# The head of a two-layer attention kernel: the second image's statistics and norm moved ahead in the order of work

## The chip, the cores and the metric

The kernel runs on one core of one Trainium2 chip. The metric is the device time of one execution in microseconds (us). Before the change it was 2573.52 us, the median of three runs (2573.21 to 2574.76).

The core's engines work side by side, each through a queue of its own: PE is the matmul engine (its weight loads are listed as PEld), DVE the vector engine, ACT the scalar engine, POOL the general engine, and SP issues most of the transfers between the chip's memory and the core's.

## What is computed

Two attention layers over a batch of eight images of 512 channels by 1024 pixels, the second on the first one's output. The first layer, cut to what matters:

```python
h = group_norm(xf, gn_w, gn_b)                   # 32 groups of 16 channels
qkv = jnp.einsum('oc,bct->bot', qkv_w, h) + qkv_b[None, :, None]
q, k, v = jnp.split(qkv.reshape(b * NUM_HEADS, -1, T), 3, axis=1)
q, k, v = fake_quant(q), fake_quant(k), fake_quant(v)   # 8 bits, range over the whole tensor
w = softmax(jnp.einsum('bct,bcs->bts', q * scale, k * scale))
a = jnp.einsum('bts,bcs->bct', w, v)
return xf + jnp.einsum('oc,bct->bot', proj_w, a.reshape(b, c, T)) + proj_b[None, :, None]
```

The second layer is a group norm, one head of attention over 512 channels, a projection and the residual. Since `fake_quant` needs the smallest and the largest value of q, k and v over all images, the kernel first computes q, k and v of all eight images and stores them. This is its phase 1, and it takes until about 580 us. The change lies in its first hundred microseconds.

## The kernel before

**Precision.** [...] Weights and x are therefore split into `high`, `low` and `mix`, three tiles of the fast type: `high` by ACT, then `low` (a subtraction) and `mix` (one fused operation) by DVE. For the weights a further ACT operation scales `low`. `split_half(b, hf)` gives the six steps of an image's half, three for each half of the channels: ACT, DVE, DVE. `split_weights` gives `first` (ACT), `second` (both DVE operations) and `third` (ACT). The list `parts` holds four of these: `parts[0]` for half of the q weights, `parts[1]` for half of the k weights, and `parts[2]` and `parts[3]` for v. The split of an image takes the buffer of an earlier one: two are kept, and `raw_w`, the unsplit weights, is in the first.

**A block.** `three` runs twelve matmuls into two PSUM banks: `w_high` by `high` and `w_low` by `low` into bank `a`, and the `mix` pair into bank `m`. `put` brings them out: for q and k, ACT scales `a` into one of three `u` tiles and DVE joins `u` with `m` and takes the largest value; for v, DVE does both. After two blocks `store` takes the smallest value on DVE (TENSOR_REDUCE) and issues the store. The `ps_1` pool has eight banks for everything in phase 1.

**Image 0.** Some of its q and k is done directly in fp32 by `qk_mm` (the tiles `early`, `late` and `last`), while the splits are being made; `out_of` brings these out with the bias and `keep` stores them. What remains are eight blocks for each half of its pixels: two of q, two of k, four of v (`blocks`, the branch `b == 0`). The other images have twelve blocks a half.

**The biases.** The norm's offset goes through the weights into the biases. `bias(i)` is a generator in two steps for q, k and v (`bq`, `bk`, `bv`). Its first step runs eight narrow matmuls into `wt` and copies them to `stage` on ACT; its second sums them by matmuls (`wc` for q and k, `wr` for v) and adds on DVE.

**The norm of the following images.** `norm_steps` takes statistics of each of four channel groups on DVE (two BATCH_NORM_STATS2 and one aggregate, then a `yield`), averages the means over the groups by a matmul (`gps`), forms offsets on DVE, averages these by a second matmul (`gps2`), and forms scale and offset on DVE with a power on POOL between. `apply` then scales x in place on ACT, a channel group at a time.

**The order.** In phase 1 the calls on DVE and ACT are tied in the order in which the program makes them (`InOrder`), and so are the matmuls (`mm`). So the text is the order of each of the three queues, for images 0 and 1; from image 2 on DVE and ACT are placed by the compiler's scheduler, and SP's transfers always are. The head is written out call by call, and after it the loop over images and halves runs a block and then gives each generator in `side` one step (`go`). In image 0's first half these are `chores`, which has the rest of `bv`, the stores of `last` and the last steps of `second`, and `every_second(ahead)`, which takes one step of image 1's norm on every second block: four statistics in eight blocks. In the second half `ahead` goes on, a step a block, and after the third block it is drained and the split of image 1's first half begins, a step a block. What is left of `side` at the end of a half is drained.

The lines the change and the steps of the prediction touch are the function `norm`, the statements from `first = split_half(0, 0)` to `next(bv)`, the generators after it, and the loop `for b in range(B)`.

Of the kernel before, what the change touches and what calls it, by code (L numbers as in the profile page):

```python
# [19 lines left out]
B, C, HH, WW = 8, 512, 32, 32  # L20
T = HH * WW
CC = C // P
NT = T // P
NH = T // 512
# [34 lines left out]
def attn_pair_kernel(  # L59
# [12 lines left out]
    class InOrder:  # L72
# [10 lines left out]
        def after(self, ins):  # L83

            tc.add_manual_dep(self.latest, ins.name, IN_ORDER, reason="order")
# [69 lines left out]
    dve, act, pe = InOrder(nc.vector), InOrder(nc.scalar), InOrder(nc.tensor)  # L155
# [52 lines left out]
    def mm(ps, lhsT, rhs, **kw):  # L208
        ins = nc.tensor.matmul(ps, lhsT=lhsT, rhs=rhs, **kw).ins  # L209
        part = lhsT.shape[-1] / P if lhsT.shape[-1] in (32, 64) else 1.0  # L210
        if rhs.dtype in (BF, F16, F32R):
            part *= 0.25 * lhsT.shape[0] / P
        pe.t += math.prod(rhs.shape[1:]) * 1.677e-3 * part
        if last_mm[0] is not None:
            tc.add_manual_dep(ins, last_mm[0].name, IN_ORDER, reason="order")
        last_mm[0] = ins

    def stat_tiles(n, nm):
        return (
            small.tile([P, n, NH, 6], F32, tag=f"gst{n}", name=f"gst_{nm}"),  # L220
            small.tile([P, n, 2], F32, tag=f"gmv{n}", name=f"gmv_{nm}"),
        )

    def aggregate(mv, st, i):
        dve.bn_aggr(mv[:, i, :], st[:, i, :, :].rearrange("p a s -> p (a s)"))
# [81 lines left out]
    with ExitStack() as fast:  # L307
# [84 lines left out]
        with tc.tile_pool(name="p1w", bufs=1) as p1w, tc.tile_pool(  # L392
# [7 lines left out]
            xs, halves = {}, {}  # L400
# [43 lines left out]
            def split_half(b, hf):  # L444
                halves[b, hf] = t = p1.tile(
                    [P, 3, CC, 512], F32R, tag="half", name=f"half_{b}_{hf}"
                )
                steps = []
                for k in (slice(0, CC // 2), slice(CC // 2, CC)):
                    high, low, mix = (t[:, i, k, :] for i in range(3))  # L450
                    src = xs[b][:, k, bass.ts(hf, 512)]
                    steps += [
                        lambda high=high, src=src: act.activation(
                            high, src, AF.Identity, scale=NUDGE
                        ),
                        lambda high=high, low=low, src=src: dve.tensor_tensor(
                            low, src, high.bitcast(F32), ALU.subtract
                        ),
                        lambda high=high, low=low, mix=mix: dve.scalar_tensor_tensor(
                            mix, low.bitcast(F32), -SH, high.bitcast(F32), ALU.mult, ALU.add  # L460
                        ),
                    ]
                return steps
# [3 lines left out]
                    step()  # L467
                    yield

            def norm(b):  # L470

                xt = xs[b]

                def apply(cc, scale, off):
                    act.activation(xt[:, cc, :], xt[:, cc, :], AF.Identity, bias=off, scale=scale)

                return norm_steps(
                    lambda cc, hf: xt[:, cc, bass.ts(hf, 512)], None, V_GN0W, one, f"a{b}",
                    fine=True, apply=apply,
                )  # L480

            out_ring = wa.rearrange("p s k n -> p (s k n)")
# [5 lines left out]
            def turn_of(name, n):  # L488
                turns[name] += 1
                return (turns[name] - 1) % n  # L490

            def out_tile():
                i = turn_of("out", 3)
                return out_ring[:, i * 1024 : (i + 1) * 1024].rearrange("p (a n) -> p a n", a=2)
# [73 lines left out]
            def bias(i):  # L568


                by_channel, by_row = weigh(
                    one, stage[i % 2][:, 512:1024] if i == 0 else stage[1][:, 0:512],
                    lambda e: raw_w[:, e, bass.ts(i, C)], gbb, f"{i}",
                )
                yield
                if i == 2:
                    dve.tensor_add(vb, vb, by_row())
                    dve.tensor_scalar(vrow, vb, -SH, None, ALU.mult)
                    return
                cols = bass.ts(i, PAIRS)  # L580
                dve.tensor_add(
                    qkb[:, cols], by_channel(),
                    vec[:, V_QKB + i * PAIRS : V_QKB + (i + 1) * PAIRS],
                )
                dve.tensor_scalar(qkbt[:, cols], qkb[:, cols], -SH, None, ALU.mult)
# [7 lines left out]
            ]  # L593
            eps = p1w.tile([P, 1], F32, name="eps")
            dve.memset(eps, EPS)

            def cols0(c):
                return [t[:, c : c + 1] for t in tiny]
# [35 lines left out]
            def qk_mm(ps, t, hf, cc):  # L634
                mm(
                    ps[hf], lhsT=raw_w[:, cc, bass.ts(t, P)],
                    rhs=x0[:, cc, bass.ts(hf, 512)], start=(cc == 0), stop=(cc == CC - 1),
                )
# [23 lines left out]
            bq, bk, bv = (bias(i) for i in range(3))  # L662
# [6 lines left out]
            second = []  # L669
# [45 lines left out]
            for t in range(2):  # L715
                for hf in range(NH):
                    out_of(early[t], outs[0], t, hf)
            next(bk, None)
            keep(outs[0], 0, 0)
            keep(outs[0], 0, 1)  # L720
            parts[0][2]()
# [1 line left out]
            parts[3][0]()  # L723
            parts[1][1]()
            parts[1][2]()
            outs.append([out_tile() for _ in range(NH)])
            last = [one(f"qkps_0_{PAIRS + 1}_{hf}") for hf in range(NH)]
            for hf in range(NH):
                for cc in range(CC):
                    qk_mm(last, PAIRS + 1, hf, cc)  # L730
            for hf in range(NH):
                out_of(late, outs[1], PAIRS, hf)
            parts[2][1]()
            parts[2][2]()
            parts[3][1]()
            parts[3][2]()
            second.extend(split_half(0, 1))
            for step in second[:3]:
                step()
            for hf in range(NH):  # L740
                out_of(last, outs[1], PAIRS + 1, hf)
            next(bv)

            def chores():
                keep(outs[1], 1, 0)
                next(bv, None)
                yield
                keep(outs[1], 1, 1)
                yield from one_by_one(second[3:])
# [24 lines left out]
            def every_second(it):  # L774
                for _ in range(CC):
                    yield
                    go(it)
                    yield

            def blocks(b, hf):  # L780
                if b == 0:
                    yield from qk_block(b, hf, 0, 1)
                    yield from qk_block(b, hf, 1, 1)
                    for n in range(2):
                        yield from v_block(b, hf, n)
                    return
                for m in (1, 0):
                    yield from qk_block(b, hf, 0, m)
                    yield from qk_block(b, hf, 1, m)
                    yield from v_block(b, hf, m)  # L790

            for b in range(B):
                for hf in range(NH):
                    if hf == 0:
                        ahead = norm(b + 1) if b + 1 < B else iter(())
                        if b == 0:
                            side = [chores(), every_second(ahead)]
                        else:
                            side = [one_by_one(split_half(b, 1)), every_second(ahead)]
                            if b == 1:  # L800
                                side.insert(0, split_rest())
                            if b == B - 1:
                                load_folded("h", (NQ1, NK1))
                    else:
                        if b == 0:
                            load_rest()
                        if b + 2 < B:
                            load_x(b + 2)
                        if b == B - 1:
                            load_folded("v", (NV1, WP1))  # L810
                        side = [ahead]
                    n = 0
                    for _ in blocks(b, hf):
                        for g in side:
                            go(g)
                        n += 1
                        if hf == 1 and b + 1 < B and n == (4 if b else 3):
                            for _ in ahead:
                                pass
                            side = [one_by_one(split_half(b + 1, 0))]  # L820
                    for g in side:
                        for _ in g:
                            pass
                InOrder.planned = b == 0
# [1461 lines left out]
```

## Time and profile before

| | |
|---|---|
| time, median of three runs | 2573.52 us |
| profiled execution, its own time | 2572.91 us |
| its span, first to last instruction | 2570.9 us |
| mean granted clock of PE | 0.996 |
| PE busy, 0 to 20 / 20 to 41 / 41 to 60 us | 9.13 / 20.89 / 16.20 us |
| PE busy, 60 to 75 / 75 to 93 / 93 to 111 us | 15.00 / 15.15 / 15.56 us |
| DVE busy, 41 to 60 / 60 to 75 / 75 to 93 us | 16.27 / 14.61 / 11.01 us |
| granted clock of PE, 75 to 93 / 93 to 111 us | 0.81 / 0.92 |

The page gives busy time by engine and by groups of instructions. The other views are taken from the same execution: what each engine waited for in a stretch, the instructions in order of time, and a table by stretches. In the order of time a row has its start, its duration, the engine, the line, the operation, what it writes and reads, its shape and its count; in brackets stands how long the engine had been idle before it and which instruction ended that. All of DVE's and ACT's operations have the line of the helper that records them (L91), and the matmuls that of theirs (L209), so that they are told apart by their tiles. Consecutive rows of the same kind are merged into one. Successive operations of one engine overlap by about 0.1 us, so that their spacing is taken from start to start.

From 120 us on PE is busy without a break to the end of phase 1 (67.00 of 67.00 us in each image from 177 to 513 us).

### The profile page before, as it was taken

What the parts mean: (1) busy time and instruction counts of PE and PEld (TensorE: products, weight loads), DVE (VectorE), ACT (ScalarE), POOL (GpSimd) and SP (SyncE); (2) the same over time, 40 slices, a digit from 0 to 9 for tenths busy, and PEclk for the clock granted to TensorE, in tenths of its full rate; (3) what the DMA queues carried; (4) which work ended last, traced back from release to release, by engine and by line L of the source; (5) the groups of instructions that cost most, each with busy time, mean ns of one, the idle gap of its engine ahead of it and who ended that gap; (6) DMA issues with size and microseconds to landing.
All of it is one profiled execution on the core that took longest, in us unless ns stands there. A gap on an engine that the chain in (4) does not pass through costs nothing.

```text
span 2570.9 us, 38729 instructions
## 1 busy us (share of the span) xinstructions
PE 2522.9 (98%) x15670; PEld 1749.2 (68%) x15670; DVE 1897.0 (74%) x2747; ACT 1347.9 (52%) x1685; POOL 188.3 (7%) x167
## 2 busy tenths in 40 slices
PE   7999999999999999999999999999999999999998
PEld 4788888883257756775777577657756775777787
DVE  6788777668887778777777787777778777875544
ACT  3222222218857665665667466746665675664121
POOL 0000000001110001000100100010001000100000
PEclk9999999999999999999999999999999999999999
DMA  4343333336722232123223222322232123212211
GB/s 168 135 146 135 114 117 128 125 130 158 185 83 71 71 115 91 46 79 124 83 68 106 84 87 61 112 101 67 73 114 91 54 71 124 91 47 83 86 38 39
DMA packets 160717, 250.70 MB, mean 98 GB/s; under 512 B 27152, under 2 KB 93712, under 8 KB 159120
## 3 DMA queue, kind: packets, MB, share of 16 engines
q1 hardware_dynamic: 125792, 182.81, 21.8%
q10 hardware_dynamic: 30560, 57.71, 6.5%
q0 software_dynamic: 4176, 7.60, 1.6%
q8 instruction: 125, 2.05, 0.3%
q14 instruction: 64, 0.52, 0.1%
HBM read 153.64 MB, written 86.28 MB: 93 GB/s over the span
## 4 chain that ended last, share of the span: by engine, by line
PE 85%; DVE 4%; issue 3%; ACT 2%; DMA 1%; POOL 0%; ACTq 0%; SPq 0%; DVEq 0%; POOLq 0%
PE s L209 15%; PE o L209 14%; PE qkps L209 12%; PE pj L209 9%; PE av L209 8%; PE v2ps L209 7%; PE g L209 6%; PE vps L209 6%; PE st L209 4%; PE sm L209 3%; DVE two L91 1%; ACT pt L91 1%; DMA two<-spare 1%; DVE acc L91 0%; DVE h L91 0%
## 5 line engine op out<-in xcount | busy, mean ns | idle before, releaser
L91 ACT ACTIVATE pt<-st,esc 128x1024 f32<-128x1024 f32 x467 | 497.0, 1114 | 332.1 <-PE st L209 316.2
L91 DVE TENSOR_TENSOR two<-pt,two 128x1024 f16<-128x1024 f32 x467 | 561.7, 1217 | 133.2 <-POOL two L1073 101.9
L91 ACT CAST two<-pt 128x1024 f16<-128x1024 f32 x346 | 350.8, 1055 | 8.5 <-ACT p L91 5.1
L1073 POOL CAST two<-pt 128x1024 f16<-128x1024 f32 x112 | 148.6, 1326 | 1408.7 <-PE sm L209 736.1
L209 PE MATMUL av<-two,v 128*32 128x512 f16 x3968 | 246.8, 382 | 3.3 <-DVE two L91 2.8
L209 PE MATMUL s<-g,h 128*128 128x256 f32 x1024 | 233.4, 380 | 0.0
L209 PE MATMUL pj<-ao,wp 128*128 128x512 f32 x512 | 223.6, 595 | 0.0
L209 PEld LDWEIGHTS s<-g,h 128*128 128x128 f32 x1024 | 192.9, 190 | 31.0 <-issue 4.3
L91 ACT ACTIVATE u_ring<-qkps,qkbt 128x512 f32<-128x512 f32 x89 | 61.1, 687 | 253.0 <-PE qkps L209 228.5
L209 PEld LDWEIGHTS <-v 128*32 128x32 f16 x3968 | 91.9, 96 | 141.8 <-issue 68.9
L209 PE MATMUL s<-g,sums 128*128 128x256 f32 x768 | 178.5, 381 | 0.2 <-DVE p L91 0.2
L209 PEld LDWEIGHTS pj<-ao,wp 128*128 128x128 f32 x512 | 96.1, 190 | 121.3 <-issue 113.4
L209 PE MATMUL o<-p,v 128*128 128x256 f32 x768 | 175.2, 382 | 1.0 <-DVE p L91 1.0
L209 PE MATMUL st<-q,k 64*128 64x512 bf16 x1024 | 163.7, 383 | 11.6 <-ACT pt L91 7.2
L209 PEld LDWEIGHTS o<-p,v 128*128 128x128 f32 x768 | 144.3, 190 | 27.1 <-issue 5.7
L209 PEld LDWEIGHTS s<-g,sums 128*128 128x128 f32 x768 | 144.6, 190 | 24.5 <-issue 4.6
L209 PE MATMUL sm<-two,ones 128*32 128x512 f16 x1984 | 136.5, 380 | 0.0
L209 PE MATMUL qkps<-half,w_low 128*128 128x512 f32 x480 | 131.9, 397 | 2.0 <-DVE half L91 2.0
L209 PE MATMUL qkps<-half,w_high 128*128 128x512 f32 x480 | 133.8, 401 | 0.0
L209 PE MATMUL qkps<-half,w_mix 128*128 128x512 f32 x480 | 132.3, 398 | 0.4 <-DVE half L91 0.4
L209 PEld LDWEIGHTS <-k 64*128 64x128 bf16 x1024 | 34.7, 94 | 143.7 <-issue 141.6
L209 PE MATMUL v2ps<-wm,h 128*128 128x256 f32 x512 | 119.9, 383 | 1.9 <-ACT g L91 1.3
(226 smaller groups left out, 3906.4 us busy)
## 6 DMA issues: line engine op xcount, KB each, us to landing
rs<-rs_d SPq DMA_DIRECT2D x76, 256.0 KB
x<-in_x_dram SPq DMA_DIRECT2D x32, 512.0 KB
q_d<-wa SPq DMA_DIRECT2D x32, 512.0 KB
k_d<-wa SPq DMA_DIRECT2D x32, 512.0 KB
v_d<-v_ring SPq DMA_DIRECT2D x32, 512.0 KB
raw<-q_d SPq DMA_DIRECT2D x32, 512.0 KB
raw<-k_d SPq DMA_DIRECT2D x32, 512.0 KB
x_d<-h SPq DMA_DIRECT2D x64, 256.0 KB
```

What stands on the lines that cost most here:

```text
L91: ins = self.latest = op(*args, **kw).ins
L209: ins = nc.tensor.matmul(ps, lhsT=lhsT, rhs=rhs, **kw).ins
L1073: copy(two[:, 0], pt)
```

## The change

`next(bk, None)`, the k bias's second step, is moved from ahead of the two `keep` of `outs[0]` to behind the split of `parts[1]`. `next(bv)`, the v bias's first step, is moved from the end of the head to directly behind the last fp32 matmuls. The first ACT step of the split of image 0's second half is put between the two last steps of `parts[3]`, and its two DVE steps behind `out_of(last)`.

The statistics of image 1, `stats1`, are taken in the head: channel group 0 ahead of `out_of(last)`, groups 1 to 3 at the end. `norm` is given them as `mv` and leaves its own out. In image 0's first half the norm is stepped by the new generator `after(4, ahead)`: nothing for four blocks, then its empty first step, the first averages on block 6, nothing on block 7, the second averages on block 8. The split of image 1's first half begins after the first block of image 0's second half, no longer after the third. The other images keep their order.

```diff
-            def norm(b):
+            def norm(b, mv=None):
...
-                    fine=True, apply=apply,
+                    fine=True, mv=mv, apply=apply,
...
+            st1, mv1 = stat_tiles(CC, "a1")
+
+            def stats1(c):
+                for hf in range(NH):
+                    dve.bn_stats(st1[:, c, hf, :], xs[1][:, c, bass.ts(hf, 512)])
+                aggregate(mv1, st1, c)
...
-            next(bk, None)
             keep(outs[0], 0, 0)
             keep(outs[0], 0, 1)
             parts[0][2]()
...
             parts[3][0]()
             parts[1][1]()
             parts[1][2]()
+            next(bk, None)
             outs.append([out_tile() for _ in range(NH)])
             last = [one(f"qkps_0_{PAIRS + 1}_{hf}") for hf in range(NH)]
             for hf in range(NH):
                 for cc in range(CC):
                     qk_mm(last, PAIRS + 1, hf, cc)
+            next(bv)
             for hf in range(NH):
                 out_of(late, outs[1], PAIRS, hf)
             parts[2][1]()
             parts[2][2]()
             parts[3][1]()
+            second.extend(split_half(0, 1))
+            second[0]()
             parts[3][2]()
-            second.extend(split_half(0, 1))
-            for step in second[:3]:
-                step()
+            stats1(0)
             for hf in range(NH):
                 out_of(last, outs[1], PAIRS + 1, hf)
-            next(bv)
+            second[1]()
+            second[2]()
+            for c in range(1, CC):
+                stats1(c)
...
+            def after(n, it):
+                for _ in range(n):
+                    yield
+                for k, _ in enumerate(it):
+                    yield
+                    if k == 1:
+                        yield
...
-                        ahead = norm(b + 1) if b + 1 < B else iter(())
+                        ahead = norm(b + 1, None if b else mv1) if b + 1 < B else iter(())
                         if b == 0:
-                            side = [chores(), every_second(ahead)]
+                            side = [chores(), after(4, ahead)]
...
-                        if hf == 1 and b + 1 < B and n == (4 if b else 3):
+                        if hf == 1 and b + 1 < B and n == (4 if b else 1):
```

## The prediction

> **What bounds the kernel now.** I read the page first for the bound of the whole, then what the matmul engine waited for in the stretch that the change touches, then the order of time around each of those waits.
>
> ```profile
> span 2570.9 us, 38729 instructions
> ...
> PE 2522.9 (98%) x15670; PEld 1749.2 (68%) x15670; DVE 1897.0 (74%) x2747; ACT 1347.9 (52%) x1685; POOL 188.3 (7%) x167
> ```
>
> PE is busy 98% of the span, so only what lets PE idle or run slowly can be won, at most some 48 us in all. The waits of PE from 49 to 112 us, its whole way through image 0's blocks and the first block of image 1, are three entries:
>
> ```profile
> PE gps_a L209 <- DVE gmv_a L91: 2.9, 1, 2.9
> PE wr L209 <- ACT stage L91: 2.8, 1, 2.8
> PE qkps L209 <- DVE half L91: 2.4, 2, 2.0
> ```
>
> The same view from 111 to 580 us, the rest of phase 1, has 0.8 us of PE waiting, and the chain of waits starts at 110 us and then lies on PE: what is won before 110 us is won for the kernel, unless something later stops being covered. The timeline of PE shows the price of each wait:
>
> ```profile
> 55.19 1.13 PE L209 MATMUL wr<-stage,fourth 128*128 128x512 f32 x2 [2.80 <-ACT stage L91]
> 55.75 1.49 PE L209 MATMUL qkps<-half,w_high 128*128 128x512 f32 x4
> ...
> 81.38 0.59 PE L209 MATMUL gps_a<-gmv_a,gavg 128*128 128x4 f32 x2 [2.85 <-DVE gmv_a L91]
> 81.83 2.05 PE L209 MATMUL qkps<-half,w_high 128*128 128x512 f32 x4
> 83.68 1.91 PE L209 MATMUL qkps<-half,w_low 128*128 128x512 f32 x4
> ...
> 107.88 0.97 PE L209 MATMUL qkps<-half,w_low 128*128 128x512 f32 x2 [2.00 <-DVE half L91]
> 108.64 1.05 PE L209 MATMUL qkps<-half,w_mix 128*128 128x512 f32 x2
> 110.14 1.22 PE L209 MATMUL qkps<-half,w_mix 128*128 128x512 f32 x2 [0.44 <-DVE half L91]
> 111.16 1.31 PE L209 MATMUL qkps<-half,w_high 128*128 128x512 f32 x4
> ```
>
> After the second and third wait four matmuls take 1.7 us from start to start, not 0.92. The table of stretches says why: the granted clock is 0.50 from 81.4 to 87 us and from 109 to 111.
>
> Last, the vector engine at the end of the head:
>
> ```profile
> 41.49 0.16 DVE L91 TENSOR_TENSOR qkb<-wc,vec 128x4 f32<-128x4 f32 x1 [4.72 <-PE wc L209]
> ...
> 41.76 2.34 DVE L91 TENSOR_REDUCE rcs<-wa 128x1 f32<-128x1024 f32 x2
> ...
> 54.70 1.23 DVE L91 TENSOR_TENSOR half<-x,half 128x1024 fp32r<-128x1024 f32 x1 [2.07 <-ACT half L91]
> ```
>
> DVE idles 4.7 us for a small sum and 2.1 us for a copy on ACT, and is then busy without a break to 83 us. That is the queue in which PE's second wait has its cause.
>
> [...] 2.85 us of idling led to 5 us at clock 0.50, the 2.80 us before `wr` to none. [...]
>
> **The change, part by part.** I number image 0's blocks 1 to 8 (first half) and 9 to 16; block 17 is image 1's first. A qk block lasts 2.75 us at full clock, a v block 2.80 (starts 90.38 to 93.12, 93.12 to 95.92).
>
> *What PE loses now.* First wait: block 1 starts at 49.35, block 3 at 58.91; block 1's own 2.87, `wr`'s 0.53 and block 2's 2.75 make 6.15, so 3.4 are lost. Second: 2.85 idle, and from 81.38 to 88.55 (7.17) it does four groups of 0.92 and two averages of 0.12, 3.9 in all: 3.25 lost to the clock, 6.1 together. Third: block 17 lasts from 104.32 to 111.16, 6.84 for 2.75, and block 18's first group 1.14 for 0.93: 4.3. Sum 13.8 us.
>
> *DVE in the head.* `next(bk)` goes behind the two minima and the split of the k weights. They fill the 4.7 us of waiting. From 36.7, with start-to-start times of the rows above and their neighbours: minima 2.26, split 2.39, to 41.35; the sum is ready at 41.49 as before, +0.27; `out_of(late)` 1.34; splits 2.40 + 2.40, to 47.9. `stats1(0)` costs 1.44 (62.98 to 64.41): 49.34. `out_of(last)` 1.34 (its matmuls end at 48.42): 50.68. `second[1]` needs ACT's `second[0]`.
>
> *ACT in the head.* `next(bv)` puts the copy of `wt` ahead of `parts[2][2]`, `second[0]` and `parts[3][2]`, which queue behind it. PE's order doesn't change (nothing of PE stood between), `wt` ends at 49.41, the copy at 50.0, not 55.1. Then 0.96 each: `second[0]` ends at 51.95. So `second[1]` starts 1.3 us after DVE is free, 51.97 instead of 54.70; it and `second[2]` take 2.40, the three other statistics 4.32: 58.69. DVE begins block 1's `put` at 58.69, now at 58.44: the four statistics (5.8 us) have been put in at a cost of 0.25.
>
> *First wait.* `wr` needs the copy (50.0) and is reached at 52.2. It goes, block 3 starts at 55.5, and PE is 3.4 us earlier.
>
> *Second wait.* From block 1's `put` on, DVE's order is that of now without four times 1.44. Now the row from 58.44 to 81.25, less 5.76, is 17.05; with the offsets (0.5) and the last part of the norm (1.58, with the 1.1 us wait for POOL's power) DVE is at 77.8 when block 8 is stored. PE unhindered: block 5 at 61.0, block 6 ends at 66.6, averages 0.12, block 8 ends at 72.3, second averages, block 9 at 72.5. The first averages find their data long done. The second need the offsets, which stand behind block 6's `put` on DVE: 58.69 + 13.08 = 71.77, +0.5 = 72.27. That is even with PE's 72.3; I take 0.1, between 0 and 1.5 us. Behind this matmul all of PE waits, as it does now. No averages are left in the second half.
>
> *The scalings.* `after(4, ...)` lets `apply(0)` fall on block 8, and the loop then drains the other three: four on ACT in a row from 77.75, 1.15 each (three in 3.50), to 82.35, all ahead of block 9's `u`. DVE waits for that from 78.9 to 83.0. PE is then in block 12: blocks 9 to 12 hold all eight banks, and block 13 wants one at 83.5; `u` of block 9 frees it at 83.0. Half a microsecond to spare: nothing, but up to 1.5 us if DVE is late.
>
> *Third wait.* The split of image 1's first half starts after block 9, no longer after block 11, one step a block, ending at 15 (now behind 16). DVE from 83.0: `put` 9, 10 (0.61 each), store 1.1, 11, step 1.15, 12, step 1.15, store 1.1, v `put` 13 (1.44), 14, step 1.15 to 94.0, store, 15, last step to 97.7. PE reaches block 17 at 94.7 and its second `mix` pair at 97.0: 0.7 us wait remains, between 0 and the 4.3 of now.
>
> *DMA.* No DMA is added. The second half's first split reads an x that has been on chip since about 24 us (DMA is at rest from 24 to 28). The stores of k leave earlier. SP's loads of `rest` need the `wr` matmuls and `vrow` (52.8 and 61.5), of image 2 the end of DVE's read at 66: each about where it is.
>
> *What follows.* At block 18 DVE is about 1.7 us further behind PE than now; now it idles 2.3 us at 112 to 114, which takes it. I count no loss after.
>
> Sum: 13.8 − 0.1 − 0.7 = 13.0, rounded down to 12.9 for the times that start to start leaves out. The profiled execution has 2572.91 (span 2570.9 and 2.0 around it), 0.6 under the median, so 2560.0 there and **2560.6** against the median.
>
> **Rivals.**
> - DVE is 1.5 us later than worked out (a slower ACT chain, another bank): the second averages wait 1.5, block 17 waits 2.2 and costs 1.9 at half clock: 13.8 − 5.6 = 8.2, so 2565.3. For it: three margins of half a microsecond or less on one queue. Against: every length is measured in this very stretch.
> - The waits move whole: DVE 3 us late, the averages' wait is back at block 8 with its half clock (6.1), and block 17's (4.3). Only the first wait is won: 3.4, so 2570.1. For it: one idle of 2.0 us was enough for half clock. Against: the statistics need no more than the 6.8 us that DVE idles in the head.
> - Slower: from image 2 on the order of DVE and ACT is not written out but left to the scheduler's own clock, which the head moves. If it then places norm or split one block later in each of the six images that follow, each pays block 17's 4.3: 25.8 − 12.9 = +12.9, so 2586.4. It decides from four images on (17.2 against 12.9). Against: from 177 to 580 DVE waits some 100 us for PE, so a block's delay is covered.
> - The change does less than it says: eight steps in the half are just enough for averages at 6 and 8; were they one step late, the drain would still run them before block 9, with the offsets' wait of rival one.
>
> **How the numbers follow.** Forecast 0.63, first rival and the fourth 0.21, second 0.09, slower 0.05, other small outcomes 0.02. The range takes in no wait at all (13.8, and a microsecond of scatter: 2558.5) and the first rival with a further 2 us: 2558.5 to 2567.3. A measurement of this kernel can tell about 0.2%, 5.1 us: faster is forecast and first rival, 0.84; the second rival and the rest are within, 0.1; slower 0.06.
>
> **What would show it.** `wr` right behind block 1; no wait for `gmv_a`; clock 1.00 from 78 to 96 us; `gps_a` on `gd_a` within 0.5 us of block 8's end; four scalings in a row on ACT near 78 to 82; block 18 near 98 us, not 111. I would be wrong if block 18 starts early and the span doesn't follow, or if clock 0.50 returns anywhere before 100 us.

## The result and the profile after

The changed kernel takes 2560.39 us, the median of five runs (2559.32 to 2562.17), against 2573.21 us of the kernel before beside it (median of five, 2568.38 to 2574.76). The ratio is 0.9956 with a 95% interval from 0.9942 to 0.9971, a gain of 7 to 15 us. The prediction was 2560.6. Timed once more, in another set, the changed kernel took 2560.86 (five runs, 2559.77 to 2562.02) and the kernel before 2571.45 (nine runs, 2568.36 to 2573.33): 0.9960, from 0.9947 to 0.9974.

The page of the changed kernel, its first lines:

```profile
span 2557.2 us, 38727 instructions
...
PE 2515.9 (98%) x15670; PEld 1746.2 (68%) x15670; DVE 1897.6 (74%) x2747; ACT 1346.5 (53%) x1685; POOL 186.0 (7%) x167
```

The same matmuls are counted, and PE's busy time is 7 us shorter: four matmuls that last 1.08 us at full clock last 1.91 at half clock, so lost clock is counted as busy. (A part of the 7 us is a stretch of half clock at 702 us, of which more below.) What PE waited for from 36 to 112 us is now one entry (columns: in total, times, longest, in us):

```profile
PE qkps L209 <- DVE half L91: 1.0, 1, 1.0
```

And PE's order of time at the places where it waited before, and at block 17 (`...` stands for rows left out):

```profile
52.38 1.02 PE L209 MATMUL wr<-stage,fourth 128*128 128x512 f32 x2
52.83 1.49 PE L209 MATMUL qkps<-half,w_high 128*128 128x512 f32 x4
54.16 1.08 PE L209 MATMUL qkps<-half,w_low 128*128 128x512 f32 x4
...
67.08 0.28 PE L209 MATMUL gps_a<-gmv_a,gavg 128*128 128x4 f32 x2
...
72.90 0.28 PE L209 MATMUL gps_a<-gd_a,gavg 128*128 128x4 f32 x2
...
97.19 0.62 PE L209 MATMUL qkps<-half,w_mix 128*128 128x512 f32 x2
98.78 0.74 PE L209 MATMUL qkps<-half,w_mix 128*128 128x512 f32 x2 [0.97 <-DVE half L91]
99.36 1.08 PE L209 MATMUL qkps<-half,w_high 128*128 128x512 f32 x4
```

From 36 to 112 us one row alone has a bracket, the last `mix` pair of block 17. The averages, for which PE stood 2.85 us and then ran 6.3 us at half clock (0.50 from 81.38 to 87.72), run where PE meets them. Block 18 begins at 99.36, where it began at 111.16. The granted clock is 1.00 from 73 to 98 us.

One difference of times is not enough to read a change of 0.4% by, so I read three stretches of each trace by landmarks of PE: from block 1's first matmul to block 18's, from block 1's to the first `fold` matmul after phase 1, and from there to the end.

| kernel | block 1 to 18 | block 1 to `fold` | rest | its time |
|---|---|---|---|---|
| before | 61.81 | 530.64 | 1990.9 | 2572.91 |
| changed | 49.85 | 518.45 | 1989.2 | 2559.32 |
| difference | 11.96 | 12.19 | 1.7 | 13.59 |

The three columns don't add up to the last: the stretch ahead of block 1 is 0.16 us longer in the changed kernel, and what lies outside the span differs by 0.1.

The change won 12.2 us. The 1.7 us of the rest can't be put down to it: over all thirteen profiles of this study that stretch lies between 1989.2 and 1992.4 us, whatever the head is, and the two profiles of the changed kernel lie at 1989.2 and 1992.0. In the profile of before, PE's clock is 0.77 and 0.81 in two stretches of 4 us from 700 to 708 us, and in that of the changed kernel 1.00 there. The second profile of the changed kernel has that dip as well (0.61 and 0.54 from 688 to 696 us, the same place some 13 us earlier), so the dip comes and goes with one and the same head.

### The profile page after: what moved, and what is told of

Read it like the earlier page. It is cut to its first block, busy times and chain, and to the rows that moved or that the text cites. A ratio compares the mean times of both kernels' runs of the same rounds, so it can differ in the third digit from the quotient of the medians.

```text
span 2557.2 us, 38727 instructions
## 1 busy us (share of the span) xinstructions
PE 2515.9 (98%) x15670; PEld 1746.2 (68%) x15670; DVE 1897.6 (74%) x2747; ACT 1346.5 (53%) x1685; POOL 186.0 (7%) x167
## 4 chain that ended last, share of the span: by engine, by line
PE 85%; DVE 5%; ACT 2%; issue 1%; DMA 1%; POOL 0%; SPq 0%; ACTq 0%; DVEq 0%
PE s L209 15%; PE o L209 13%; PE qkps L209 12%; PE pj L209 8%; PE av L209 8%; PE v2ps L209 7%; PE vps L209 6%; PE g L209 6%; PE st L209 4%; PE sm L209 3%; DVE two L91 2%; ACT pt L91 1%; PE fold L209 1%; DVE h L91 1%; DVE acc L91 0%
```

## The experiments

My theory: PE lost 13.8 us in three waits, two of which were followed by half clock; DVE's queue sets the last two, ACT's the first; and DVE's 4.7 us of waiting in the head is what pays for taking the statistics early. The rivals: one part of the change does it all, or others add nothing; or the slow matmuls have nothing to do with the waits.

Up to "The scalings spread" each kernel was executed once. In the order of the sections the times are 2566.41, 2563.74, 2572.50, 2561.79, 2563.54, 2560.26 and 2558.01 us; the kernel before, executed once beside the first four and once beside the others, took 2568.54 and 2569.71. Since executions of the kernel before differ by 6.4 us among themselves, I read the stretches of the traces and not these times.

### The filled hole alone

```diff
-            next(bk, None)
             keep(outs[0], 0, 0)
...
             parts[1][2]()
+            next(bk, None)
```

> The kernel before with one edit: the k bias's second step goes behind the split of the k weights. My theory: DVE's 4.7 us of waiting in the head is filled, so ACT's copy for the v bias ends near 50.5 and PE's first wait is gone; block 1's put starts near 53.8, the statistics in the blocks end near 76.6, so PE waits about 1.3 us for the first averages and about 0.5 for the second; image 1's split still starts late, so block 17 still waits up to 2.4. Block 18 starts between 103 and 107 us. Rival, the filled hole alone is the gain: block 18 near 99.4 us as with the whole change. Rival, the v bias's copy has to be moved for the first wait to go: PE still waits 2 us or more before wr.

Measured: block 18 at 104.20 us, block 1 to 18 in 55.10 us, to `fold` in 525.29: 5.35 us won, under half of the whole. PE's order of time:

```profile
51.97 1.02 PE L209 MATMUL wr<-stage,fourth 128*128 128x512 f32 x2
...
77.08 0.38 PE L209 MATMUL gps_a<-gmv_a,gavg 128*128 128x4 f32 x2 [1.84 <-DVE gmv_a L91]
77.32 1.18 PE L209 MATMUL qkps<-half,w_high 128*128 128x512 f32 x4
...
100.92 1.22 PE L209 MATMUL qkps<-half,w_low 128*128 128x512 f32 x2 [2.26 <-DVE half L91]
...
104.20 1.91 PE L209 MATMUL qkps<-half,w_high 128*128 128x512 f32 x4
```

The first wait is gone although the v bias's copy stands where it stood: with DVE 4.7 us earlier at the splits, ACT has done with them early enough, and the copy ends at 50.83. So the second rival falls. The statistics in the blocks still make PE wait 1.84 us (1.3 expected), this time at full clock after it (1.00 from 76 to 79 us); the second averages don't wait (0.5 expected); block 17 waits as before, here 2.26 us, and half clock follows (0.50 from 101 to 104 us). The first rival falls too: the filled hole isn't the whole.

### All but the filled hole

The same edit backwards, on the changed kernel.

> The changed kernel with the k bias's second step back in its old place. My theory: DVE stands 4.7 us again and is about 3.1 us later at block 1's put (62.0); the copy on ACT is early still, so PE has no wait before wr; the second averages wait about 2.8 us for the offsets and may bring half clock (up to 3.2 more), block 17 waits 1 to 3. Block 18 between 102 and 107 us. Rival, the early statistics and the moved averages do the work and the filled hole adds nothing: block 18 within 1 us of 99.4.

Measured: block 1's `put` at 61.35 us, 12.58 after block 1's first matmul (9.37 in the changed kernel), so DVE is 3.2 us later. Block 18 begins at 102.05, within the range expected and not within 1 us of 99.4, so the rival falls. Block 1 to `fold` takes 521.89: 3.4 us of the gain are lost.

```profile
72.37 1.20 PE L209 MATMUL vps<-w_mix,half 128*128 128x512 f32 x4 [0.73 <-DVE u_ring L91]
75.13 0.39 PE L209 MATMUL gps_a<-gd_a,gavg 128*128 128x4 f32 x2 [1.55 <-DVE gd_a L91]
75.37 1.27 PE L209 MATMUL qkps<-half,w_high 128*128 128x512 f32 x4
76.44 1.91 PE L209 MATMUL qkps<-half,w_low 128*128 128x512 f32 x4
```

DVE's delay comes out in two places: 0.73 us in block 8, where PE waits for DVE to read out an earlier v block (from 36 to 115 us no other run has a wait of that kind), and 1.55 at the second averages, 2.3 together (2.8 expected), with half clock after it (0.55 from 77 to 80 us). Block 17 has no wait (1 to 3 expected): counted from block 1, PE reaches it 4.7 us later than in the changed kernel, and DVE's last step of the split is only 3.2 later.

### Half clock by itself

The kernel before, with matmuls in the place where PE stood:

```diff
         yield
+        if warm is not None:
+            warm()
         ps = bank(f"gps_{nm}")[:, 0:n]
...
+            def keep_busy():
+                ps = one("busy")
+                for i in range(12):
+                    mm(
+                        ps, lhsT=wsp[0][:, i % CC, C // 2 : C // 2 + P], rhs=halves[0, 1][:, 0, i % CC, :],
+                        start=(i == 0), stop=(i == 11),
+                    )
...
```

> The kernel before with twelve matmuls more (2.75 us), whose result nobody reads, ahead of the first averages, where PE stood 2.85 us: PE is busy while it waits. The computation is otherwise complete. My theory: the wait still costs its 2.8 us, but the clock stays at 1.00 from 81 to 88 us, which was half of the price: the 3.25 us of slow matmuls are gone, and block 18 starts near 108 us or earlier, not at 111.2. Rival, the slow matmuls had another cause (the two small averages, a clash of memory): four matmuls still take 1.7 us there and block 18 starts at 111.

Measured, PE's order of time:

```profile
78.25 2.91 PE L209 MATMUL busy<-half,w_high 128*128 128x512 f32 x12
81.26 0.38 PE L209 MATMUL gps_a<-gmv_a,gavg 128*128 128x4 f32 x2
81.51 1.17 PE L209 MATMUL qkps<-half,w_high 128*128 128x512 f32 x4
82.52 1.08 PE L209 MATMUL qkps<-half,w_low 128*128 128x512 f32 x4
...
107.37 0.80 PE L209 MATMUL qkps<-half,w_mix 128*128 128x512 f32 x2 [1.06 <-DVE half L91]
107.96 1.91 PE L209 MATMUL qkps<-half,w_high 128*128 128x512 f32 x4
```

The averages come no earlier than in the kernel before (81.26 and 81.38), since DVE is no earlier, but the next four matmuls take 1.01 us from start to start, not 1.85, and the clock is 1.00 from 78 to 90 us. From block 1 to block 17 it is 52.05 us against 54.97: 2.9 us won by keeping PE busy with nothing, and block 18 begins at 107.96, as expected. The rival, another cause of the slow matmuls, falls. At block 17 most of that is paid back: DVE isn't earlier there either, so PE waits 2.27 and 1.06 us, half clock follows (0.61 from 107 to 111 us), and up to `fold` only 1.7 us stay. By its time, 2572.5 us, the execution is no faster than those of the kernel before; its rest, 1992.4, is the longest of the thirteen.

### Averages on neighbouring blocks

```diff
-                for k, _ in enumerate(it):
-                    yield
-                    if k == 1:
-                        yield
+                for _ in it:
+                    yield
```

> The changed kernel with the averages on blocks 6 and 7, without the empty step between. My theory: PE reaches the second averages at 70.1 us while the offsets are ready at 72.5: a wait of about 2.4 us, with half clock after it or not; the scalings come a block earlier, and block 17's wait of 1.0 goes since PE is later. Block 18 near 100.6 us at full clock, near 103.5 with half clock. Rival, the distance is of no account: no wait at the averages, block 18 within 0.5 us of 99.4 or earlier.

Measured: a wait of 2.41 us at the second averages, and then

```profile
71.61 0.39 PE L209 MATMUL gps_a<-gd_a,gavg 128*128 128x4 f32 x2 [2.41 <-DVE gd_a L91]
71.86 1.75 PE L209 MATMUL vps<-w_high,half 128*128 128x512 f32 x4
73.40 1.91 PE L209 MATMUL vps<-w_low,half 128*128 128x512 f32 x4
```

The clock is 0.71 from 71 to 74 us and 0.73 from 74 to 77. Block 18 begins at 101.25 (between the 100.6 expected at full clock and the 103.5 at half), 52.78 us after block 1, and block 17 has no wait. Block 1 to `fold` is 521.31, 2.9 us more than in the changed kernel: the empty step is worth that. The rival falls.

### The split begun later

```diff
-                        if hf == 1 and b + 1 < B and n == (4 if b else 1):
+                        if hf == 1 and b + 1 < B and n == (4 if b else 3):
```

> The changed kernel with the split of image 1's first half beginning after block 11, as in the kernel before. My theory: DVE reaches the split's last two steps only after block 16's put, so block 17 waits about 2.3 us for low and 0.5 for mix, with up to 1.5 us of half clock; from block 1's start to block 18's start it is 51.5 to 53.0 us (49.85 in the changed kernel, 61.81 before). Rival, the third wait was only a consequence of the second one and goes by itself: within 0.5 us of 49.85.

Measured, PE's order of time in block 17:

```profile
98.34 0.74 PE L209 MATMUL qkps<-half,w_low 128*128 128x512 f32 x2 [2.00 <-DVE half L91]
...
100.60 1.21 PE L209 MATMUL qkps<-half,w_mix 128*128 128x512 f32 x2 [1.06 <-DVE half L91]
```

The clock is at half into block 18 (0.58 from 100 to 104 us), and it is 52.63 us from block 1 to 18 and 521.99 to `fold`: 3.5 us more than in the changed kernel. The third wait was not a consequence of the second, which is away here.

### The v bias's first step in its old place

```diff
                     qk_mm(last, PAIRS + 1, hf, cc)
-            next(bv)
...
             for c in range(1, CC):
                 stats1(c)
+            next(bv)
```

> The changed kernel with the v bias's first step back at the end of the head. My theory after the first runs: with DVE's hole filled, ACT is done with the splits by 51.4 us and the copy ends near 52.0, just before PE reaches wr at 52.4: no wait or under 0.3 us; and since ACT's split of the second half no longer stands behind the copy, DVE doesn't wait 1.35 us for it, block 1's put starts near 57.5 and block 17 waits 0 to 0.3 instead of 0.97. From block 1's start to block 18's 48.5 to 49.0 us. Rival, the prediction's own step that the moved copy is what removes the first wait: PE waits 1 us or more before wr and the stretch is 50.5 or longer.

Measured: no wait before `wr`, none at block 17; 48.64 us from block 1 to 18, 517.26 to `fold`, 1.2 us *less* than in the changed kernel. ACT's order of time, first the changed kernel's:

```profile
49.70 0.59 ACT L91 COPY stage<-wt 128x512 f32<-128x512 f32 x1 [7.03 <-PE wt L209]
50.18 1.06 ACT L91 ACTIVATE w_low<-w_low 128x1024 fp32r<-128x1024 f32 x1
51.15 1.04 ACT L91 ACTIVATE half<-x 128x1024 fp32r<-128x1024 f32 x1
```

Then with the step back in its place:

```profile
46.03 1.06 ACT L91 ACTIVATE w_low<-w_low 128x1024 fp32r<-128x1024 f32 x1 [3.11 <-DVE w_mix L91]
49.90 1.06 ACT L91 ACTIVATE half<-x 128x1024 fp32r<-128x1024 f32 x1 [2.81 <-PE wt L209]
50.86 1.05 ACT L91 ACTIVATE w_low<-w_low 128x1024 fp32r<-128x1024 f32 x1
51.81 0.57 ACT L91 COPY stage<-wt 128x512 f32<-128x512 f32 x1
```

The copy ends at 52.38 us, 2.62 after block 1's first matmul and just ahead of `wr` (2.89 after it). In the changed kernel it ends 2.1 us sooner than needed, and holds up the `w_low` and the `half` behind it, for which DVE then stands 1.35 us; here DVE goes on to that step at once. So beside the other parts this one costs a little.

### The scalings spread

```diff
-                            for _ in ahead:
-                                pass
-                            side = [one_by_one(split_half(b + 1, 0))]
-                    for g in side:
+                            if b:
+                                for _ in ahead:
+                                    pass
+                                side = []
+                            side.append(one_by_one(split_half(b + 1, 0)))
+                    for g in side[: 1 if (b, hf) == (0, 0) else None]:
```

> The changed kernel with image 1's last three scalings not in a row at the end of the first half but one on each of blocks 9 to 11, beside the split. My theory: block 9's u is no longer behind four scalings, so DVE doesn't stand 4.15 us there and reaches the last step of the split about 1 us earlier; block 17's wait of 0.97 goes. From block 1's start to block 18's 48.5 to 49.1 us. Rival, DVE's standing is covered and wins nothing, since the put of each block then waits for its own u: 49.5 or more.

Measured: 48.60 us from block 1 to 18, 516.84 to `fold`, 1.6 less than in the changed kernel; PE waits nowhere from 36 to 115 us. This is what DVE met at block 9 in the changed kernel:

```profile
83.47 0.69 DVE L91 CUSTOM_DVE_ANT_0 wa<-qkps,u_last 128x512 f32<-128x512 f32 x1 [4.15 <-ACT u_last L91]
```

and with the scalings spread:

```profile
79.43 0.69 DVE L91 CUSTOM_DVE_ANT_0 wa<-qkps,u_last 128x512 f32<-128x512 f32 x1 [0.75 <-ACT u_last L91]
...
81.14 0.69 DVE L91 CUSTOM_DVE_ANT_0 wa<-qkps,u_ring 128x512 f32<-128x512 f32 x1 [1.01 <-ACT u_ring L91]
...
83.79 0.69 DVE L91 CUSTOM_DVE_ANT_0 wa<-qkps,u_ring 128x512 f32<-128x512 f32 x1 [0.70 <-ACT u_ring L91]
```

The 4.15 us of standing become 2.5 in three pieces. The rival was right that each block's `put` now waits for its own `u`, and wrong that this wins nothing.

### Both, and the repeats

The kernel with the last two edits together, timed in five rounds:

> The changed kernel with both of the last two edits: the v bias's first step at the end of the head, and the scalings spread over blocks 9 to 11. My theory: each alone took away block 17's wait, so both together win no more on PE: from block 1's start to block 18's 48.6 us, with DVE about 2 us further ahead of need; the time is 1.2 us under the changed kernel's, which five rounds hardly tell from the same, and some 11 to 13 us under before. Rival, DVE's lead is worth more later (image 1's blocks): the stretch from block 18 to the first matmul after phase 1 gets shorter than 468.6 us.

Measured: 48.62 us from block 1 to 18, 516.84 to `fold`: together they win no more than the spread scalings alone, since each takes away the same wait, block 17's. So with the scalings spread the moved v bias costs nothing. From block 18 to `fold` it is 468.2 us, 0.4 less than in the changed kernel; but the spread scalings alone have that too, so the longer lead that the rival spoke of adds nothing. Its time is 2559.22 us (2558.53 to 2560.30), 0.9956 of before with an interval from 0.9942 to 0.9969; the changed kernel beside it:

> The changed kernel again on the same chip as the last, timed in five rounds. My theory: the stretch from block 1's start to block 18's is 49.85 us again, the time 10 to 13 us under before.

49.85 us and 518.45 us, each the same as the first time to the last digit; 2560.86 us, 0.9960. The version with both edits is 1.6 us under the changed kernel by median, as the stretch to `fold` is; the intervals of the two ratios overlap almost wholly, so by times alone it isn't shown.

No experiment put the early statistics alone back into the blocks, or the step of the second half's split that was moved forward on ACT. Nearest to it is the filled hole alone: with the statistics on every second block the last of them is ready only at 77.08 us, ten microseconds behind the place of the first averages in the changed kernel (67.08).

The kernel before, for the scatter of its times:

> The kernel before once more, for its profile: runs of it differ by up to 6 us (2568.4 to 2574.8). My theory: PE's three waits are the same to 0.2 us, while the half clock after them comes and goes with the moment: from block 1's start to block 18's between 56 and 62 us, the difference to 61.81 all in matmuls at half clock. Rival, the scatter is elsewhere: 61.8 within 0.3 us.

> The kernel before a third time, for where its scatter of 6 us lies; both profiles so far are of executions near 2573 us. My theory: if this execution is near 2569, the stretch from block 1 to the first matmul after phase 1 (530.6 and 531.9 so far) is 2 to 5 us shorter for less half clock. Rival, the scatter lies after phase 1: the stretch is 530.6 or more and the rest (1990.9 and 1990.3) shorter by 3.

Neither gave what I expected. The first of the two took 2573.92 us and has 61.82 us from block 1 to 18, the rival's value; only to `fold` is it 1.3 us longer (531.90), as block 18 ran at half clock too (0.50 from 111 to 114 us). The other took 2571.38, with 61.80, 530.09 and 1990.2. No execution near 2568.4 was profiled, so where that one gains 3 us more is open.

## Why the prediction was right, point by point

The trace of the changed kernel at the places that the forecast names, first DVE's, then ACT's:

```profile
58.88 0.69 DVE L91 CUSTOM_DVE_ANT_0 wa<-qkps,u_ring 128x512 f32<-128x512 f32 x1
...
72.44 0.16 DVE L91 TENSOR_TENSOR gd_a<-gd_a,gmv_a 128x4 f32<-128x4 f32 x1
...
97.51 1.22 DVE L91 SCALAR_TENSOR_TENSOR half<-half 128x1024 fp32r<-128x1024 f32 x1
...
78.22 4.64 ACT L91 ACTIVATE x<-x,goff_a,grstd_a 128x1024 f32<-128x1024 f32 x4 [16.76 <-DVE goff_a L91]
```

- **That the gain is PE's three waits and the clock after them.** Held. Part by part, from one landmark of PE to the next, before and changed: block 1 to block 3, 9.56 and 6.49, 3.07 won; block 3 to 17, 45.41 and 39.32, 6.09; block 17, 6.84 and 4.04, 2.80; block 18 to `fold`, 0.23. Sum 12.19, where 12.9 was forecast.
- **The first wait, 3.4 us.** It was 3.07. The mis-sized term is `wr`: I gave it 0.53 us and counted the slow four matmuls behind it (1.33 us from start to start, not 0.92) as lost. They take 1.33 in the changed kernel too, without a wait and at clock 1.00, so that time goes with the fp32 matmul ahead of them: its two records take 0.45 us to the next start and those four 0.41 more, 0.86 together, and eight such fp32 records in the head of the kernel before take 3.52 (44.83 to 48.35), 0.88 for two.
- **What removes it.** Incomplete. The prediction gave it to the moved copy. That is enough (with the k bias back, `wr` doesn't wait), but not needed: filling DVE's hole alone removes it as well. With both done, and the scalings in a row, the moved copy costs 1.2 us.
- **DVE in the head.** Block 1's `put` was forecast at 58.69 and came at 58.88, with PE's block 1 itself 0.16 later: the sum of rows held to some hundredths.
- **The second wait, 6.1 us.** 6.09. The offsets were forecast for 72.27 and PE for 72.3. They came at 72.60 and 72.90: no wait, by 0.3 us. This margin is as thin as it looked: without the filled hole PE waits 1.55 us there, without the empty step 2.41.
- **The scalings.** Forecast from 77.75 to 82.35, DVE standing from 78.9 to 83.0. Measured 78.22 to 82.86 and a stand of 4.15 us to 83.47. PE didn't wait for a bank at block 13 (84.13).
- **The third wait, 0.7 us left.** It was 0.97, and block 17 took 4.04 for 2.75: 1.29 lost. DVE's last step came at 98.73, not 97.7. Half of that is there at block 9's `put` (83.47 for 83.0), and 0.51 is a stand of DVE in block 14 whose cause the trace doesn't show. This is the larger of the two mis-sized terms: 3.0 us were won here (2.80 in block 17, 0.23 behind it) where 3.6 were forecast. The other is `wr`.
- **That nothing is lost after block 18.** Held: 468.83 us to `fold` before, 468.60 after, so the slower rival, a late norm or split in each later image, did not come.
- **The bound of the whole.** "At most some 48 us" is the time in which PE is not busy, and so leaves out what is lost at half clock, which counts as busy: 7 us of busy time went without a matmul less. And after the third wait no four matmuls take 1.7 us: a pair takes 0.76 from start to start (107.88 to 108.64), the clock falling in the middle of it (1.00 up to 108.2 us, 0.50 from there to 111). Neither reading enters the sum.

The forecast of 12.9 us and the 12.8 between the two medians agree so well by luck: the trace has 12.2, the second set of runs 10.6, within the same interval, and executions of the kernel before differ by 6.4 us.

## What to carry to other kernels

An engine that stands in an in-order queue for a small result leaves time that can pay for work needed later: here 4.7 us of DVE, and some of the 2.1 us that it stood for ACT, took in 5.8 us of statistics, and that, with the averages moved to where their inputs are ready, removed two of PE's waits and 1.5 us of the 2.4 in the third. A short wait of PE can cost twice its length if half clock follows (2.85 us cost 6.1), so small waits are worth removing. Of several moves made together, each should be tried backwards: one of these cost 1.2 us, which the whole hid.

## What was not expected

Half clock did not follow the length of the wait alone. The 2.79 to 2.81 us before `wr` were followed by full clock in all four profiles that have that wait, and the 2.85 to 2.87 us before the averages by half clock in all three of the kernel before. The prediction had both from one trace; that each came out the same way every time was new. These and other waits, with the clock behind them:

| kernel, wait | PE's clock after it |
|---|---|
| before, 2.80 us before `wr` | 1.00 from 55 to 59 us |
| before, 2.85 us before the averages | 0.50 from 81.38 to 87.72 |
| before, 2.00 us in block 17 | 1.00 to 108.2, 0.50 from there to 111 |
| split begun later, 2.00 us in block 17 | 1.00 to 100, half clock after a further 1.06 us of waiting (0.58 from 100 to 104) |
| filled hole alone, 1.84 us before the averages | 1.00 from 76 to 79 |
| filled hole alone, 2.26 us in block 17 | 0.50 from 101 to 104 |
| half clock by itself, 2.27 us in block 17 | 1.00 from 104 to 107, half clock after a further 1.06 us (0.61 from 107 to 111) |
| all but the filled hole, 0.73 us in block 8, then 1.55 before the second averages | 0.55 from 77 to 80 |
| neighbouring blocks, 2.41 us before the second averages | 0.71 from 71 to 74, 0.73 from 74 to 77 |
| changed, 0.97 us in block 17 | 1.00 from 99.5 to 110 |

In the kernel before, the 2.00 us in block 17 had half clock behind them, and the 2.80 us before `wr` had none. What decides between them these runs don't show: no run moved a wait and changed nothing else.
